# Strassen's form for a layer's last matrix product, and its normalization in pairs of chunks

## The chip, the cores and the metric

The kernel runs on one core of a Trainium2 chip. The metric is the device time of one execution in microseconds (us), as the median of the runs. The engines of the core are TensorE (PE in the profile; PEld is its weight load), VectorE (DVE), ScalarE (ACT), GpSimd (POOL) and SyncE (SP, which here only issues DMAs). Each engine has a queue of its own and works through it in order; engines wait for each other on semaphores.

## The reference, cut to what matters

Four layers run one after the other on an image tensor x of 2 images, 512 channels and 32 x 32 positions, all in float32. Layer 0 is a deformable attention with an MLP, layer 1 an attention over channels with a batch normalization, layer 2 a softmax attention over positions, layer 3 a gate and a non-local block. The change lies in layer 1, in how its output is made and normalized:

```python
K = conv1x1(X, Wq, bq).reshape(b, HEADS, d, n)
Q = conv1x1(X, Wk, bk).reshape(b, HEADS, d, n)
V = conv1x1(X, Wv, bv).reshape(b, HEADS, d, n)
M = jnp.einsum('bhmn,bhen->bhme', K, V)
Out = jnp.einsum('bhme,bhmn->bhen', M, Q)
Out = conv1x1(Out.reshape(b, c, h, w), Wo, bo) + X
mean = Out.mean(axis=(0, 2, 3), keepdims=True)
var = Out.var(axis=(0, 2, 3), keepdims=True)
Out = (Out - mean) * jax.lax.rsqrt(var + EPS)
return Out * gamma[None, :, None, None] + beta[None, :, None, None]
```

There is no softmax in it, so all that acts on X can be folded into one 512 x 512 matrix per image: Out = A X + bias + X.

## The kernel before, in words

x is held in SBUF as four chunks (k, 0 to 3) of 128 channels, each with 2048 columns: image 0's 1024 positions and then image 1's. A matmul takes 128 x 128 weights and 512 columns. It is float32, and the profile has two records for one such matmul. A PSUM bank holds one 128 x 512 result.

Layer 0 ends with the MLP. Its two products already have the form that the change brings to layer 1: helper functions form sums of blocks (`differences` at L967 for the weights, `spreads` at L974 for the activations), `product` (L1090 to L1106) runs seven block products into four banks A to D, and small reader functions take the banks up as they fill. Its last instructions on VectorE are L1161 (a bank is added to x) and L1165 (the last sum into x, with the bias, and with the sums over positions that layer 1 needs).

Layer 1 (L1209 to L1373) then computes, for each image b:

- G, the 512 x 512 matrix X X^T. L1235 transposes 128 positions at a time into PSUM (`pt`), L1240 (VectorE) and L1242 (ScalarE) copy them out by turns (`xt`), L1244 multiplies (`pg`). L1252 to L1257 copy the upper triangle out and mirror it.
- `bvs` from the position sums (L1262, L1270), U = G Wv (matmul L1278, read at L1285), M per head (matmul L1293, read at L1302).
- R from M and Wk (matmul L1316, read at L1317), a bias row (L1319 to L1334), and A = R Wo (matmul L1339, copied at L1342). The five weight matrices wq, wv, wk, wo and wo in another layout (`wot`, `won`) lie in one tile `lw`.
- The last product (L1348): for each of four output chunks o and each of four column blocks t of 512, four matmuls over k into one bank, and L1355 on VectorE, which adds the bias and x and writes x2. These are 64 matmuls.
- The batch normalization: for each chunk, L1363 takes statistics of four column blocks, L1365 joins them, L1367 to L1372 make scale and shift (the square root, L1368, on ScalarE), and L1373 scales the whole chunk in place.

Layer 2 starts with `l2_fg` (L1388, `pf`): for each of two outputs and two column halves, four matmuls over the chunks of the normalized x of image 0, read by ScalarE (L1395). Then `l2_attn` goes over eight tiles of positions: scores (L1421, `pscore`), a maximum (L1432), an exponential (L1435), a scaling (L1436, L1437), transposes (L1441), copies (L1442); `l2_h` (L1407, `ph`) is put between them. L1450 (`pz`) needs all eight tiles.

The queues aren't in the order of the source. When the program is built, a scheduler goes by what is ready and places each instruction in its engine's queue; afterwards that order is fixed. Statistics of one chunk, for instance, come between the sums of the next.

Of the kernel before, what the change touches and what calls it, by code (L numbers as in the profile page):

```python
# [10 lines left out]
F32 = mybir.dt.float32  # L11
AF = mybir.ActivationFunctionType
ALU = mybir.AluOpType
# [3 lines left out]
P = 128  # L17
# [54 lines left out]
def conv_seq(  # L72
# [61 lines left out]
    with ExitStack() as ctx_l0:  # L134
# [459 lines left out]
        with tc.tile_pool(name="hid", bufs=3) as hid, tc.tile_pool(name="sm", bufs=1) as sm, tc.tile_pool(name="hps", bufs=2, space=PSUM) as hps, tc.tile_pool(  # L594
# [6 lines left out]
            def at(n, when, fn, *args):  # L601

                todo.setdefault((n, when), []).append((fn, args))
# [615 lines left out]
    with tc.tile_pool(name="d", bufs=2) as d, tc.tile_pool(name="dpg", bufs=4, space=PSUM) as dpg, tc.tile_pool(  # L1219
# [66 lines left out]
        for b in both:  # L1286

            M[b] = d.tile([P, KC, 2, DH], F32, name="M")
            nc.gpsimd.memset(M[b], 0.0)  # L1289
            pm = dps.tile([P, KC, 2, DH], F32, name="pm", tag="ps")  # L1290
            for o in range(KC):
                for k in range(KC):
                    nc.tensor.matmul(  # L1293
                        pm[:, o].rearrange("p h e -> p (h e)"),
                        lhsT=wq[:, k, o * P : (o + 1) * P],
                        rhs=U[b][:, k, o * P : (o + 1) * P],
                        start=(k == 0),
                        stop=(k == KC - 1),
                    )
                for h in range(2):  # L1300
                    hs = slice(h * DH, (h + 1) * DH)
                    nc.vector.scalar_tensor_tensor(  # L1302
                        M[b][hs, o, h, :],
                        bvs[b][hs, o, h, :],
                        v("L1_conv_bq", o)[hs],
                        pm[hs, o, h, :],
                        ALU.mult,
                        ALU.add,
                    )
        for b in both:  # L1310
            R = d.tile([P, KC, C], F32, name="R")
            prb = dps.tile([P, C], F32, name="prb", tag="ps")
            for o in range(KC):
                mo_ = M[b][:, o].rearrange("p h e -> p (h e)")
                pr = dps.tile([P, C], F32, name="prk", tag="ps")
                nc.tensor.matmul(pr, lhsT=mo_, rhs=wk[:, o, :], start=True, stop=True)  # L1316
                (nc.vector.tensor_copy, nc.scalar.copy)[o % 2](R[:, o, :], pr)  # L1317

                nc.tensor.matmul(  # L1319
                    prb[:, o * P : (o + 1) * P],  # L1320
                    lhsT=v("L1_conv_bk", o).to_broadcast([P, P]),
                    rhs=mo_,
                    start=True,
                    stop=True,
                )
            rb = d.tile([P, C], F32, name="rb")
            nc.scalar.copy(rb, prb)
            bias1[b] = d.tile([P, KC], F32, name="bias1")
            for o in range(KC):
                junk = d.tile([P, C], F32, name="junk", bufs=1)  # L1330
                nc.vector.scalar_tensor_tensor(
                    junk, won[:, o, :], 1.0, rb, ALU.mult, ALU.mult, accum_out=bias1[b][:, o : o + 1]
                )
            nc.vector.tensor_tensor(bias1[b], bias1[b], v("L1_conv_bo"), ALU.add)  # L1334
            A[b] = d.tile([P, KC, C], F32, name="A")
            for i in range(KC):
                pa = dps.tile([P, C], F32, name="pa", tag="ps")
                for k in range(KC):
                    nc.tensor.matmul(  # L1339
                        pa, lhsT=R[:, k, i * P : (i + 1) * P], rhs=wot[:, k, :], start=(k == 0), stop=(k == KC - 1)  # L1340
                    )
                (nc.vector.tensor_copy, nc.scalar.copy)[i % 2](A[b][:, i, :], pa)  # L1342
        for o in range(KC):
            for t in range(NT // 512):
                b, ns = t // 2, slice(t * 512, (t + 1) * 512)
                pr = (dps, dpg)[t % 2].tile([P, 512], F32, name="pr", tag="ps g".split()[t % 2])
                for k in range(KC):
                    nc.tensor.matmul(  # L1348
                        pr,
                        lhsT=A[b][:, k, o * P : (o + 1) * P],  # L1350
                        rhs=x[:, k, ns],
                        start=(k == 0),
                        stop=(k == KC - 1),
                    )
                nc.vector.scalar_tensor_tensor(  # L1355
                    x2[:, o, ns], pr, bias1[b][:, o : o + 1], x[:, o, ns], ALU.add, ALU.add
                )
        x = x2

        for k in range(KC):  # L1360
            st = d.tile([P, NT // 512, nc.vector.BN_STATS_DIM], F32, name="st", bufs=2)
            for t in range(NT // 512):
                nc.vector.bn_stats(st[:, t, :], x[:, k, t * 512 : (t + 1) * 512])  # L1363
            mv = d.tile([P, nc.vector.BN_AGGR_DIM], F32, name="mv", bufs=2)
            nc.vector.bn_aggr(mv, st.rearrange("p t s -> p (t s)"))  # L1365
            sc = d.tile([P, 2], F32, name="sc", bufs=2)
            nc.vector.tensor_scalar(sc[:, 0:1], mv[:, 1:2], EPS, None, ALU.add)  # L1367
            nc.scalar.activation(sc[:, 0:1], sc[:, 0:1], AF.Sqrt)  # L1368
            nc.vector.reciprocal(sc[:, 0:1], sc[:, 0:1])
            nc.vector.tensor_tensor(sc[:, 0:1], sc[:, 0:1], v("L1_conv_gamma", k), ALU.mult)  # L1370
            nc.vector.tensor_tensor(sc[:, 1:2], mv[:, 0:1], sc[:, 0:1], ALU.mult)
            nc.vector.tensor_tensor(sc[:, 1:2], v("L1_conv_beta", k), sc[:, 1:2], ALU.subtract)  # L1372
            nc.vector.tensor_scalar(x[:, k, :], x[:, k, :], sc[:, 0:1], sc[:, 1:2], ALU.mult, ALU.add)  # L1373


    ctx_lw.close()
# [6 lines left out]
    def l2_fg(b, fp, ps):  # L1383
        fg = fp.tile([P, 2, HW], F32, name="fg")
        for i, half in ((0, 0), (0, 1), (1, 0), (1, 1)):
            pf = ps.tile([P, 512], F32, name="pf2", tag="ps")
            for k in range(KC):
                nc.tensor.matmul(  # L1388
                    pf,
                    lhsT=l2w[:, k, i, :],  # L1390
                    rhs=x[:, k, b * HW + half * 512 : b * HW + (half + 1) * 512],
                    start=(k == 0),
                    stop=(k == KC - 1),
                )
            nc.scalar.activation(  # L1395
                fg[:, i, half * 512 : (half + 1) * 512],
                pf,
                AF.Relu,
                bias=l2s[:, 1, 1:2] if i else l2f[:, 1:2],
                scale=l2s[:, 0, 1:2] if i else l2f[:, 0:1],  # L1400
            )
        return fg
# [332 lines left out]
```

## Time and profile before

| what | value |
|---|---|
| median of three runs | 2767.3 us (2765.76 to 2767.45) |
| profiled execution | 2764.49 us |
| its span in the profile | 2762.7 us |
| TensorE busy | 2707.0 us (98%) |
| VectorE busy | 2266.7 us (82%) |
| ScalarE busy | 1544.3 us (56%) |
| mean granted TensorE clock | 0.996 |
| layer 1, from the last L1161 to the end of its product | 2404.35 to 2583.24 us |
| its last product (L1348) | 2528.31 to 2583.24 us |

Times in the profile count from the start of the span. The busy share is an average over the whole program, most of which is layer 0's position bias (the loop of L616); what an edit in layer 1 is worth has to be read from layer 1's own stretch.

### The profile page before, as it was taken

The numbers are of one execution on the slowest core, as the hardware profiler recorded it, in microseconds if no ns is written. First come the engines' busy times: TensorE is split into PE (matmuls) and PEld (weight loads), VectorE is DVE, ScalarE is ACT, GpSimd is POOL, SyncE is SP. The second block draws the span as 40 slices with busy tenths as digits, with TensorE's granted clock in tenths as the row PEclk, the third lists the DMA queues.
The fourth block names the chain that finished last, engine by engine and source line by source line (L and its number), as shares of the span: only waits on it lengthen the run. The fifth ranks groups of instructions, "written<-read, shape, count | busy, mean of one in ns | idle before, by whom it ended". The sixth has DMA issues, their size and how long they took to land.

```text
span 2762.7 us, 49727 instructions
## 1 busy us (share of the span) xinstructions
PE 2707.0 (98%) x19782; PEld 987.5 (36%) x19782; DVE 2266.7 (82%) x2473; ACT 1544.3 (56%) x1950; POOL 663.6 (24%) x776
## 2 busy tenths in 40 slices
PE   8999999999999999999999999999999999999996
PEld 4233323233332323333333333333344444455543
DVE  6999999999999999999999999999654545523555
ACT  6676677667667776766776676676321111001244
POOL 0333333333333333333333333333100000000000
PEclk9999999999999999999999999999999999999998
DMA  3777777777777777777787778777400000100001
GB/s 121 160 163 155 161 154 160 158 160 158 154 164 149 162 163 158 161 161 156 167 185 172 152 165 193 154 170 159 102 30 23 16 23 23 70 7 0 0 1 61
DMA packets 145479, 335.14 MB, mean 121 GB/s; under 512 B 22592, under 2 KB 32064, under 8 KB 144480
## 3 DMA queue, kind: packets, MB, share of 16 engines
q0 software_dynamic: 77824, 201.38, 41.1%
q1 hardware_dynamic: 66992, 130.08, 13.2%
q8 instruction: 156, 2.56, 0.4%
q14 instruction: 75, 0.61, 0.1%
q10 hardware_dynamic: 432, 0.51, 0.1%
HBM read 58.99 MB, written 4.46 MB: 23 GB/s over the span
## 4 chain that ended last, share of the span: by engine, by line
PE 93%; ACT 3%; DVE 2%; issue 1%; DMA 1%; ACTq 0%; DVEq 0%; POOL 0%; SPq 0%; POOLq 0%
PE ph L616 61%; PE A L1101 4%; PE D L1101 4%; PE C L1101 4%; PE psim L669 2%; PE pr L1348 2%; PE B L1101 2%; PE po L1036 2%; PE pg L1244 1%; PE psim L654 1%; PE pz L1450 1%; PE pa L1339 1%; PE pu L1278 1%; ACT r L625 1%; PE pscore L1421 1%
## 5 line engine op out<-in xcount | busy, mean ns | idle before, releaser
L616 PE MATMUL ph<-h,w2a 128*32 128x512 f32 x16384 | 1790.7, 593 | 7.0 <-ACT r L625 6.9
L625 ACT ACTIVATE r<-ph,sb 128x1024 f32<-128x1024 f32 x1024 | 1141.4, 1115 | 562.3 <-PE ph L616 541.1
L349 DVE CUSTOM_DVE_ANT_1 h<-tab 128x1024 f32<-128x1024 f32 x1024 | 1205.9, 1220 | 8.6 <-PE ph L616 4.7
L616 PEld LDWEIGHTS ph<-h,w2a 128*32 128x32 f32 x16384 | 533.5, 109 | 1217.5 <-issue 833.1
L631 DVE SCALAR_TENSOR_TENSOR r<-r,rel,r 128x1024 f32<-128x1024 f32 x512 | 656.0, 1281 | 28.0 <-ACT r L625 27.3
L646 POOL DMA_DIRECT2D xs<-r x512 | 476.9, 1144 | 196.0 <-PE ph L616 95.7
L634 POOL DMA_DIRECT2D r<-r x256 | 222.2, 868 | 1107.2 <-DVE r L631 931.1
L172 ACT ACTIVATE tab<-tab,vec 128x256 f32<-128x256 f32 x252 | 137.1, 544 | 0.0
L1289 POOL MEMSET M<- 128x512 f32 x2 | 1.0, 520 | 439.6 <-DVE x L1165 439.6
L1141 ACT COPY u<-A 128x512 f32<-128x512 f32 x16 | 9.4, 585 | 146.9 <-PE A L1101 146.9
L1120 ACT ACTIVATE h<-h,vec 128x512 f32<-128x512 f32 x32 | 23.1, 721 | 113.6 <-DVE h L1123 113.6
L669 PE MATMUL psim<-xs,cw 128*32 128x512 f32 x512 | 72.1, 592 | 2.1 <-DMA xs<-r 2.1
L1123 DVE TENSOR_TENSOR h<-C,u 128x512 f32<-128x512 f32 x32 | 22.1, 691 | 48.8 <-PE C L1101 48.5
L1101 PE MATMUL A<-xn,w 128*128 128x512 f32 x128 | 60.2, 593 | 0.8 <-DVE x L1043 0.8
L1101 PE MATMUL C<-hT,w 128*128 128x512 f32 x128 | 60.3, 592 | 0.0
L1101 PE MATMUL A<-h,w 128*128 128x512 f32 x128 | 60.1, 592 | 0.0
L1036 PE MATMUL po<-q,vwo 128*128 128x512 f32 x128 | 56.4, 594 | 0.0
L1348 PE MATMUL pr<-x,A 128*128 128x512 f32 x128 | 55.1, 592 | 0.0
L229 DVE SCALAR_TENSOR_TENSOR acc<-q,vec,acc 128x128 f32<-128x128 f32 (+3 forms) x88 | 46.2, 525 | 0.8
L1161 DVE TENSOR_TENSOR x<-D,x 128x512 f32<-128x512 f32 x32 | 22.1, 691 | 26.0 <-PE D L1101 26.0
L852 ACT ACTIVATE e<-e,den 128x64 f32<-128x64 f32 x128 | 41.7, 336 | 2.7 <-DVE den L848 2.7
L1161 DVE TENSOR_TENSOR x<-C,x 128x512 f32<-128x512 f32 x32 | 22.1, 690 | 24.8 <-PE C L1101 24.8
(288 smaller groups left out, 1770.3 us busy)
## 6 DMA issues: line engine op xcount, KB each, us to landing
r<-r POOLq DMA_DIRECT2D x256, 512.0 KB, 4.7
xs<-r SPq DMA_DIRECT2D x512, 128.0 KB, 2.4
xs<-r POOLq DMA_DIRECT2D x512, 128.0 KB, 4.8
tab<-fd SPq DMA_DIRECT2D x63, 512.0 KB, 6.0
lw<-in_l_w_dram SPq DMA_DIRECT2D x5, 1024.0 KB, 10.2
x<-in_x_dram SPq DMA_DIRECT2D x4, 1024.0 KB, 8.5
w<-in_mlp_w_dram SPq DMA_DIRECT2D x8, 512.0 KB, 4.2
w<-in_mlp_w_dram SPq DMA_DIRECT2D x16, 256.0 KB, 3.2
```

What stands on the lines that cost most here:

```text
L172: return nc.scalar.activation(tf, tf if src is None else src[:, :, :, ax, :], AF.Identity, bias=0.0 if ax == 0 else v("L0_conv_cpb_b1"), s ...
L229: pin(nc.vector.scalar_tensor_tensor(dst, src, wt_, dst, ALU.mult, ALU.add))
L349: nc.vector._custom_dve(TENSOR_ADD_SAT, out=h1[:, h], in0=tab[:, j, h, 0, :].unsqueeze(1).to_broadcast([P, 32, 32]), in1=tab[:, j, h, 1, : ...
L616: nc.tensor.matmul(ph[t * 32 : (t + 1) * 32, i, :], lhsT=w2a[:, o], rhs=h1s[2 * p + i][:, h, half * 512 : (half + 1) * 512], start=True, s ...
L625: pin(nc.scalar.activation(r, ph, AF.Relu, bias=sb3[:, o, 1:2]))
L631: pin(nc.vector.scalar_tensor_tensor(r0, r1, rel[:, i : i + 1], r0, ALU.mult, ALU.add))
L634: pin(nc.gpsimd.dma_start(rs[p, 0], rs.pop((p, 2)), accum_op=ALU.add))
L646: pin(nc.gpsimd.dma_start(rs[p][i::2], r[i::2, i, :], accum_op=ALU.add))
L669: nc.tensor.matmul(psims[g, kb][m * 32 : (m + 1) * 32, :], lhsT=cw3[:, 3 - i : 35 - i], rhs=rs.pop(p + m), start=False, stop=(i == 3), ski ...
L1036: nc.tensor.matmul(po, lhsT=vwo[:, k * B + t // 2, o * P : (o + 1) * P], rhs=q[:, k, ts_], start=(k == 0), stop=(k == KC - 1),)
L1101: nc.tensor.matmul(banks[bank], lhsT=a[an][k], rhs=b_[bn_][k], start=(i < 4 and k == 0), stop=(k == n - 1), skip_group_check=True,)
L1348: nc.tensor.matmul(pr, lhsT=A[b][:, k, o * P : (o + 1) * P], rhs=x[:, k, ns], start=(k == 0), stop=(k == KC - 1),)
```

## The change: what it does

For each image, A and X are cut into 2 x 2 blocks: A into blocks of 256 x 256, X into blocks of 256 channels (two chunks) by 512 columns. The four blocks of A X then come from seven block products in place of eight:

- sums of X: T1 = B12 - B11, T2 = B22 - T1, T4 = B21 - T2, T3 = B22 - B12, each 128 x 1024 in SBUF. Image 0's are put into x2's second half, which is free until image 1's results are written; image 1's into the places of wq and wv.
- sums of A, by `differences`: S1 = A21 + A22, S2 = S1 - A11, S4 = A12 - S2, and S3 = A11 - A21 in A21's place. Image 0's go into wk's place, image 1's into won's.
- `layer_out(b, o)` runs one unit of seven products of two matmuls each into four banks, for image b and for output chunks o and o + 2. There are four units, with 56 matmuls in all. Image 0 uses the four banks of one PSUM pool, image 1 those of the other.
- The readers: ScalarE copies the first product to u. VectorE adds the second to u, adds u to three blocks of x (v22, v21, v12), adds the third to v22, and writes the four result blocks with the bias to x2.

The normalization goes by pairs of chunks, (0, 2) and (1, 3), as a unit finishes two chunks at a time. Each scaling is split by image, and chunk 1 of image 0 is given to ScalarE. The first product of layer 2 takes the chunks in the order 0, 2, 3, 1. R now shares its buffers with G, and A with U.

```diff
+        lo, hi = slice(0, 2), slice(2, 4)
+        places = [x2[:, :, HW:], lw[:, 0:2].rearrange("p i k c -> p (i k c)").rearrange("p (n f) -> p n f", n=4)]
+        xblocks = {}
         for b in both:
-            R = d.tile([P, KC, C], F32, name="R")
+            b11, b21, b12, b22 = (
+                x[:, k, b * HW + t * 512 : b * HW + (t + 1) * 512] for t in range(2) for k in (lo, hi)
+            )
+            t1, t2, t3, t4 = (places[b][:, n].rearrange("p (k f) -> p k f", k=2) for n in range(4))
+            nc.vector.tensor_tensor(t1, b12, b11, ALU.subtract)
+            nc.vector.tensor_tensor(t2, b22, t1, ALU.subtract)
+            nc.vector.tensor_tensor(t4, b21, t2, ALU.subtract)
+            nc.vector.tensor_tensor(t3, b22, b12, ALU.subtract)
+            xblocks[b] = {"11": b11, "21": b21, "22": b22, "T1": t1, "T2": t2, "T3": t3, "T4": t4}
+        for b in both:
+            R = d.tile([P, KC, C], F32, name="R", tag="G")
...
-            A[b] = d.tile([P, KC, C], F32, name="A")
+            A[b] = d.tile([P, KC, C], F32, name="A", tag="U")
...
-        for o in range(KC):
-            for t in range(NT // 512):
-                b, ns = t // 2, slice(t * 512, (t + 1) * 512)
-                pr = (dps, dpg)[t % 2].tile([P, 512], F32, name="pr", tag="ps g".split()[t % 2])
-                for k in range(KC):
+        ablocks = {}
+        for b in both:
+            a11, a12, a21, a22 = (A[b][:, k, m] for m in (slice(0, C // 2), slice(C // 2, C)) for k in (lo, hi))
+            s1, s2, s4 = (
+                (wk, won)[b][:, n, :].rearrange("p (k f) -> p k f", k=2) for n in range(3)
+            )
+            differences(a11, a21, a12, a22, s1, s2, s4)
+            ablocks[b] = {"11": a11, "12": a12, "S3": a21, "22": a22, "S1": s1, "S2": s2, "S4": s4}
+
+        def layer_out(b, o):
+            pool, tag = ((dps, "ps"), (dpg, "g"))[b]
+            u = d.tile([P, 512], F32, name="u1")
+            vs = {n: d.tile([P, 512], F32, name=f"v{n}") for n in ("12", "21", "22")}
...
+            def final(n, t, other):
+                k = 2 * (int(n[0]) - 1) + o
+                nc.vector.scalar_tensor_tensor(at(n, x2), t, bias1[b][:, k : k + 1], other, ALU.add, ALU.add)
+
+            def c1(t):
+                plus(u, t, u)
+                for n in ("22", "21", "12"):
+                    plus(vs[n], u, at(n, x))
+
+            banks = {n: pool.tile([P, 512], F32, name=f"pr{n}", tag=tag) for n in "ABCD"}
+            for i, (bank, an, bn_, read) in enumerate(
+                [
+                    ("A", "11", "11", lambda t: nc.scalar.copy(u, t)),
+                    ("B", "S2", "T2", c1),
+                    ("C", "S3", "T3", lambda t: plus(vs["22"], t, vs["22"])),
+                    ("D", "S1", "T1", lambda t: final("22", t, vs["22"])),
+                    ("A", "12", "21", lambda t: final("11", t, at("11", x))),
+                    ("C", "22", "T4", lambda t: final("21", t, vs["21"])),
+                    ("D", "S4", "22", lambda t: final("12", t, vs["12"])),
+                ]
+            ):
+                for k in range(2):
                     nc.tensor.matmul(
-                        pr,
-                        lhsT=A[b][:, k, o * P : (o + 1) * P],
-                        rhs=x[:, k, ns],
-                        start=(k == 0),
-                        stop=(k == KC - 1),
+                        banks[bank],
+                        lhsT=ablocks[b][an][:, k, o * P : (o + 1) * P],
+                        rhs=xblocks[b][bn_][:, k, :],
+                        start=(i < 4 and k == 0),
+                        stop=(k == 1),
+                        skip_group_check=True,
                     )
-                nc.vector.scalar_tensor_tensor(
-                    x2[:, o, ns], pr, bias1[b][:, o : o + 1], x[:, o, ns], ALU.add, ALU.add
-                )
+                read(banks[bank])
+
+        for b in both:
+            for o in range(2):
+                layer_out(b, o)
         x = x2
 
-        for k in range(KC):
+        for ks in ((0, 2), (1, 3)):
+            scs = {}
+            for k in ks:
...
-            nc.vector.tensor_scalar(x[:, k, :], x[:, k, :], sc[:, 0:1], sc[:, 1:2], ALU.mult, ALU.add)
+            for b in both:
+                for k in ks:
+                    xs = x[:, k, b * HW : (b + 1) * HW]
+                    if (b, k) == (0, 1):
+                        nc.scalar.activation(xs, xs, AF.Identity, bias=scs[k][:, 1:2], scale=scs[k][:, 0:1])
+                    else:
+                        nc.vector.tensor_scalar(xs, xs, scs[k][:, 0:1], scs[k][:, 1:2], ALU.mult, ALU.add)
...
-            for k in range(KC):
+            for j, k in enumerate((0, 2, 3, 1)):
                 nc.tensor.matmul(
                     pf,
                     lhsT=l2w[:, k, i, :],
                     rhs=x[:, k, b * HW + half * 512 : b * HW + (half + 1) * 512],
-                    start=(k == 0),
-                    stop=(k == KC - 1),
+                    start=(j == 0),
+                    stop=(j == KC - 1),
                 )
```

More of the change, by code (lines that the diff above doesn't have):

```diff
@@ new lines, in conv_seq, with at, plus @@
+        for b in both:
[9 more added lines that the diff above has]
+            vs = {n: d.tile([P, 512], F32, name=f"v{n}") for n in ("12", "21", "22")}
+            def at(n, of):
+                m, t = int(n[0]) - 1, int(n[1]) - 1
+                return of[:, 2 * m + o, b * HW + t * 512 : b * HW + (t + 1) * 512]
+            def plus(to, t, other):
+                nc.vector.tensor_tensor(to, t, other, ALU.add)
+            def final(n, t, other):
[18 more added lines that the diff above has]
+                for k in range(2):
+                    nc.tensor.matmul(
+                        banks[bank],
[4 more added lines that the diff above has]
+                        skip_group_check=True,
+                    )
+                read(banks[bank])
@@ L1358, in conv_seq @@
+        for b in both:
+            for o in range(2):
+                layer_out(b, o)
         x = x2
-        for k in range(KC):
[L1361 to L1373, printed above, removed]
+        for ks in ((0, 2), (1, 3)):
+            scs = {}
+            for k in ks:
+                st = d.tile([P, NT // 512, nc.vector.BN_STATS_DIM], F32, name="st", bufs=4)
+                for t in range(NT // 512):
+                    nc.vector.bn_stats(st[:, t, :], x[:, k, t * 512 : (t + 1) * 512])
+                mv = d.tile([P, nc.vector.BN_AGGR_DIM], F32, name="mv", bufs=4)
+                nc.vector.bn_aggr(mv, st.rearrange("p t s -> p (t s)"))
+                sc = scs[k] = d.tile([P, 2], F32, name="sc", bufs=4)
+                nc.vector.tensor_scalar(sc[:, 0:1], mv[:, 1:2], EPS, None, ALU.add)
+                nc.scalar.activation(sc[:, 0:1], sc[:, 0:1], AF.Sqrt)
+                nc.vector.reciprocal(sc[:, 0:1], sc[:, 0:1])
+                nc.vector.tensor_tensor(sc[:, 0:1], sc[:, 0:1], v("L1_conv_gamma", k), ALU.mult)
+                nc.vector.tensor_tensor(sc[:, 1:2], mv[:, 0:1], sc[:, 0:1], ALU.mult)
+                nc.vector.tensor_tensor(sc[:, 1:2], v("L1_conv_beta", k), sc[:, 1:2], ALU.subtract)
+            for b in both:
[5 more added lines that the diff above has]
+                        nc.vector.tensor_scalar(xs, xs, scs[k][:, 0:1], scs[k][:, 1:2], ALU.mult, ALU.add)
```

## The prediction

> **What bounds the kernel now.** I read the head of the page, the chain that ended last and the costliest groups; then busy time by stage; then the timeline at the three places where the change puts work.
>
> ```profile
> span 2762.7 us, 49727 instructions
> ...
> PE 93%; ACT 3%; DVE 2%; issue 1%; DMA 1%; ACTq 0%; DVEq 0%; POOL 0%; SPq 0%; POOLq 0%
> ...
> L1101 PE MATMUL A<-xn,w 128*128 128x512 f32 x128 | 60.2, 593 | 0.8 <-DVE x L1043 0.8
> ...
> L1348 PE MATMUL pr<-x,A 128*128 128x512 f32 x128 | 55.1, 592 | 0.0
> ...
> L1161 DVE TENSOR_TENSOR x<-D,x 128x512 f32<-128x512 f32 x32 | 22.1, 691 | 26.0 <-PE D L1101 26.0
> ```
>
> TensorE carries 93% of the chain. L1348 is the product that changes: 64 float32 matmuls, two records each, with no idle time ahead of them. L1101, layer 0's MLP in the same seven-product form, runs its 128 records at the same pace, and its vector sums take 691 ns each.
>
> Busy time by stage (columns: window, its length, then PE, PEld, DVE, ACT, POOL) ahead of, in, and after the product, up to layer 2's first pz:
>
> ```profile
> 2404.35:2528.30 123.95, 122.39 (x444) 69.88 (x445) 33.17 (x70) 12.54 (x25) 0.98 (x2) 1.00 0.11 43
> 2528.30:2583.24 54.94, 54.94 (x129) 24.32 (x128) 28.48 (x51) 2.48 (x5) 0.00 (x0) 1.00 0.00 0
> 2583.24:2629.07 45.83, 43.50 (x193) 26.13 (x192) 22.19 (x41) 21.49 (x37) 0.00 (x0) 1.00 0.00 0
> ```
>
> In the product TensorE has no gap at full clock, while VectorE is busy for 28.5 of 54.9 us. So matmuls taken out shorten the stage, as long as VectorE keeps up.
>
> The timeline at layer 1's start (start, duration, engine; in brackets the idle time and who ended it):
>
> ```profile
> 2404.35 0.69 DVE L1161 TENSOR_TENSOR x<-D,x 128x512 f32<-128x512 f32 x1 [0.23 <-PE D L1101]
> ...
> 2405.07 0.75 DVE L1165 SCALAR_TENSOR_TENSOR x<-vs,vec,x 128x512 f32<-128x512 f32 x1
> 2405.09 1.53 PE L1235 MATMUL pt<-cst,x 128*128 128x128 f32 x12 [0.78 <-DVE x L1161]
> ...
> 2405.95 1.30 ACT L1242 COPY xt<-pt 128x512 f32<-128x512 f32 x2 [24.18 <-DVE x L1165]
> ...
> 2406.58 6.74 PE L1244 MATMUL pg<-xt 128*128 128x512 f32 x24
> ```
>
> ScalarE's first copy xt waits for the MLP's last L1165, and TensorE's pg for that copy.
>
> The timeline where the product ends:
>
> ```profile
> 2583.24 4.45 PE L1388 MATMUL pf<-x,l2w 128*128 128x512 f32 x10
> 2587.86 9.71 PE L1388 MATMUL pf<-x,l2w 128*128 128x512 f32 x22 [0.16 <-DVE x L1373]
> ...
> 2583.45 0.75 DVE L1355 SCALAR_TENSOR_TENSOR x<-pr,bias,x 128x512 f32<-128x512 f32 x1 [1.95 <-PE pr L1348]
> ...
> 2586.46 1.35 DVE L1373 TENSOR_SCALAR x<-x,sc 128x2048 f32<-128x2048 f32 x1
> ```
>
> Only chunk 3's normalization is left at that point, and pf on chunks 0 to 2 covers it but for about 0.3 us.
>
> The timeline at the end of layer 2's first attention:
>
> ```profile
> 2622.54 1.88 PE L1421 MATMUL pscore<-fg 128*128 128x512 f32 x4
> 2624.26 1.05 PE L1407 MATMUL ph<-l2w,x 128*128 128x128 f32 x8
> 2626.61 1.06 PE L1441 MATMUL pt<-cst,e 128*128 128x128 f32 x8 [1.29 <-DVE e L1437]
> 2628.17 1.07 PE L1441 MATMUL pt<-cst,e 128*128 128x128 f32 x8 [0.50 <-DVE e L1437]
> 2629.07 13.90 PE L1450 MATMUL pz<-at,ht 128*128 128x512 f32 x32
> ```
>
> From the last score to pz it is 4.8 us: a maximum, an exponential and a scaling in a row, with little for TensorE to do.
>
> [...] 128x1024 takes 1220 ns at L1590 and 750 ns at L1437. [...] so an early sum delays what stands behind it; the L1242 copy above shows who then waits. [...] so the one normalization given to ScalarE after Sqrt loads no table. The trace of before agrees for Relu: after Sqrt's load at 2529.11 (1.28 us) the next is at 2598.40, for the exponential.
>
> **The change part by part**, with the order in which the changed program was built.
>
> *Matmuls.* One takes 54.95/64 = 0.8585 us. 64 become 4 units of 14, 56 in all: 48.08 us. Saved: 6.87.
>
> *The image sums of b=0 (L1321 to L1324 of the changed kernel).* Four tensor_tensor of 128x1024, 1.22 each. They aren't placed beside the product but at layer 1's start: the first right after the L1161 of 2404.35, ahead of the last L1165, the second behind that. Consecutive vector instructions overlap by 0.08 (L1373 at 2558.99 lasts 1.35, the next starts at 2560.26), so L1165 comes 1.14 later, the xt copy at about 2407.1, pg at 2407.7. TensorE meanwhile does one tile of four transposes more (4 x 0.107 = 0.43), so 0.7 is lost. The second copy xt (VectorE, done at 2409.2) is in time for pg's second tile (2409.9); the other two sums stand where VectorE sits idle for 6.9 us. Bounds: 0.3 to 1.2 (all of the delay, uncovered).
>
> *The image sums of b=1*, into used wq and wv. One stands before the last U, in a 2.7 us gap. One waits for the last pm that reads wq; behind it are the last M pair and, with two more sums between, both R copies, each later by about 2 us. R's first copy ends at 2495.8, pa starts at 2496.5; the second ends at 2497.8, its matmul comes at 2498.2. Nothing lost, with 0.4 us of cover; past that each us costs one.
>
> *The sums of A.* Four of 128x512 (0.69) per image, in used wk and won. Image 0's wait for A and for prk's reads of wk; behind them stands an R copy, ending at 2514.8 where 2516.3 is needed. Image 1's start after the last copy of A (2529.1), end at 2531.9, just as VectorE is wanted for the first bank B, and TensorE is by then in image 0's banks. Nothing lost.
>
> *The reads of the products.* A unit has 5 tensor_tensor of 0.69, 4 scalar_tensor_tensor of 0.75 and 4 bn_stats of 0.69: 9.2 us in 12.02 of matmuls, and ScalarE one copy (0.59). Bank A is written again 5.2 us after its first product ends, and ScalarE copies it at once; C and D after 3.4: VectorE reads C behind four sums, done 6.9 us into the unit where the second product into C starts at 8.6. Nothing lost; PSUM banks aren't shared by the images.
>
> *The tail.* With E the end of the product: the last unit has on top four normalizations of 128x1024 (0.75) and eight small instructions, so its last sum starts at E+0.9 instead of E+0.2. Then three bn_stats and two aggregates (to E+4.1), Sqrt and the scale and shift of two chunks (0.12 to 0.2 each, to E+5.5), then chunk 1 of b=0 on ScalarE (nearest row L1587, 1.15; L1589 with a pointer scale, 1.19): done near E+6.8. TensorE has six pf matmuls on chunks 0 and 2 (5.15) and one ph (0.21), to E+5.4; next in its queue is ph on chunk 1, ahead of pf on chunk 3. It waits 1.4 us where before waited 0.3: 1.1 lost; bounds 0.5 (VectorE on time) to 1.9.
>
> *The attention behind it.* The new order sets tile 5's and 6's transposes into the middle of the last score product, so from the last score on only one ph (0.89) and one tile of transposes (0.87) lie in the same 4.8 us: idle 3.0 where before had 1.3 + 0.5. Small waits before it even out to about -0.2: 1.0 lost; bounds 0 to 2.
>
> No DMA is added, and POOL's and SP's queues are as before. Sum: -6.87 + 0.7 + 1.1 + 1.0 = -4.1. The profiled execution took 2764.49 (span 2762.7 and 1.8 around it): 2760.4, span 2758.6. The median of the runs is 2.8 above it: **2763.2**. A difference of under 0.2% (5.5 us) is about what a measurement of this kernel can't tell from none, and 4.1 is under that.
>
> **Rivals.**
> *A: the saving is kept nearly whole* (tail and attention cost nothing): 6.87 - 0.7 = 6.2, 2761.1. For: VectorE has 2.8 us free per unit, and the old tail was covered. Against: E+6.8 against E+5.4.
> *B: the tail eats more*: a wait of 3 us at ph and 2 in the attention, gain 1.6, 2765.7. For: the scale chain is all small dependent steps, and now two are interleaved. Against: the same steps took 3.0 us from sum to normalization before.
> *C: slower; VectorE becomes the bound of the product.* Its 13 instructions per unit average 0.71 us. TensorE waits from 0.92 each, the gain is gone at 1.0; at 1.2 a unit lasts 15.6 instead of 12.0: 14.4 lost, 2777.6. For: the sums now have SBUF operands on both sides while bn_stats shares the queue. Against: L1161 and L1363 hold 0.69 with TensorE at full pace.
>
> **How the numbers follow.** My forecast (2761.8 to 2764.8 by itself) 0.60, A 0.20, B 0.13, C 0.07. The range 2760.3 to 2766.0 takes in A and B and leaves out C and the ends. Faster by over 0.2% (below 2761.8): A and an edge of mine, 0.24. Slower (above 2772.8): C, 0.06. Within: 0.70.
>
> **What would show it.** Right: L1403 with 112 records in 48.1 us and no idle ahead; pg about 1.1 later against L1161; a TensorE idle of 1 to 2 us at ph released by ScalarE's L1437; one of about 3 before the last transposes. Wrong: idle ahead of L1403 released by VectorE (C), or pf running through (A); R copies late for pa would cost more than I allowed.

## The result, and the profile after

| | before | after |
|---|---|---|
| median, 20 runs each | 2766.81 us | 2761.86 us |
| lowest to highest | 2765.57 to 2768.14 | 2759.11 to 2765.84 |
| profiled execution, span | 2764.49, 2762.7 | 2765.84, 2764.0 |

The ratio of the medians is 0.9983, with a 95% interval of 0.9977 to 0.9989: the change saves 4.95 us, which is under 0.2% and still clear of none. I had forecast 4.1, a time of 2763.2 in a range of 2760.3 to 2766.0. Two things in this table are not in the forecast. The runs after spread over 6.7 us, those before over 2.6. And the profiled execution of after is the slowest of its 20: it is longer than the profiled one of before, although the kernel is faster. So stages have to be compared first.

Busy time by stage of the kernel after (columns as in the prediction): from layer 0's last sum to the product, the product, and from its end to the first pz.

```profile
2407.53:2532.22 124.69, 122.53 (x445) 69.88 (x445) 44.41 (x82) 12.46 (x25) 0.98 (x2) 1.00 0.11 43
2532.22:2580.28 48.06, 48.06 (x113) 21.28 (x112) 37.94 (x67) 4.51 (x8) 0.00 (x0) 1.00 0.00 1
2580.28:2628.56 48.28, 44.01 (x194) 27.07 (x192) 25.05 (x53) 23.32 (x39) 0.00 (x0) 0.97 0.00 1
```

Against before's 123.95, 54.94 and 45.83 these are +0.74, -6.88 and +2.45. The product is as forecast (48.08), and VectorE, 37.9 of 48.1 us busy, never makes TensorE wait in it. In the last row the granted clock is 0.97; none of before's three stages had less than 1.00. Outside of these stages layer 0 ends 3.18 us later (2407.53 against 2404.35), and pz itself takes 2.16 us more. With 0.35 less at the program's end these make up the 1.3 us by which the span is longer.

The timeline at layer 1's start:

```profile
2407.53 0.69 DVE L1161 TENSOR_TENSOR x<-D,x 128x512 f32<-128x512 f32 x1 [0.23 <-PE D L1101]
2408.14 1.21 DVE L1321 TENSOR_TENSOR x<-x 128x1024 f32<-128x1024 f32 x1
2409.27 0.74 DVE L1165 SCALAR_TENSOR_TENSOR x<-vs,vec,x 128x512 f32<-128x512 f32 x1
...
2410.13 1.07 ACT L1242 COPY xt<-pt 128x512 f32<-128x512 f32 x2 [25.19 <-DVE x L1165]
...
2410.77 1.12 PE L1244 MATMUL pg<-xt 128*128 128x512 f32 x2 [0.53 <-ACT xt L1242]
```

The first sum of X, L1321, stands ahead of the MLP's last L1165 in VectorE's queue, and L1165 starts 1.74 us behind L1161, where before it was 0.72; ScalarE's copy waits for that L1165 and TensorE's pg for the copy. From L1161 to pg it is 3.24 us; before it was 2.23.

The timeline at the product's end, E = 2580.28:

```profile
2580.28 5.31 PE L1454 MATMUL pf<-x,l2w 128*128 128x512 f32 x12
2581.04 0.74 DVE L1383 SCALAR_TENSOR_TENSOR x<-prD,bias,v 128x512 f32<-128x512 f32 x1
...
2584.80 0.27 DVE L1432 TENSOR_TENSOR sc<-vec,sc 128x1 f32<-128x1 f32 x2
2584.98 1.24 ACT L1437 ACTIVATE x<-x,sc 128x1024 f32<-128x1024 f32 x1 [0.69 <-DVE sc L1432]
...
2586.28 0.71 PE L1473 MATMUL ph<-l2w,x 128*128 128x128 f32 x4 [0.46 <-ACT x L1437]
```

ph does wait for ScalarE's normalization of chunk 1, as forecast, but not by 1.4 us: the list has 0.46, and by the starts of the matmuls 0.64 are lost (the list leaves out the overlap of 0.17 with the matmul before), where before had 0.16 in the list and 0.33 by the starts.

The timeline at the end of the first attention, and the stretches of 2 us there (the third figure from the right is the granted clock):

```profile
2622.17 1.02 PE L1487 MATMUL pscore<-fg 128*128 128x512 f32 x2
2623.03 1.05 PE L1473 MATMUL ph<-l2w,x 128*128 128x128 f32 x8
2626.82 1.94 PE L1507 MATMUL pt<-cst,e 128*128 128x128 f32 x8 [2.74 <-DVE e L1503]
2628.56 16.06 PE L1516 MATMUL pz<-at,ht 128*128 128x512 f32 x32
```

```profile
2624.00:2626.00 2.00, 0.08 (x1) 0.00 (x0) 0.89 (x4) 1.21 (x2) 0.00 (x0) 1.00 0.01 4
2626.00:2628.00 2.00, 1.18 (x6) 1.21 (x7) 0.68 (x1) 0.05 (x1) 0.00 (x0) 0.52 0.00 0
...
2632.00:2634.00 2.00, 2.00 (x5) 0.92 (x4) 0.00 (x0) 0.00 (x0) 0.00 (x0) 0.78 0.00 0
```

The idle time of 2.74 us is there as forecast. From about 2626.1, inside this gap, the clock is at half for 6.8 us, as worked out from these stretches (the two left out show 0.50): the last transposes take 1.94 us instead of 1.06, and pz 16.06 instead of 13.90. That is 3.0 us which I hadn't counted. The same happens at 46 us, in layer 0, behind a gap of 2.21 us which the kernel before has as well. The transposes behind it, before and after:

```profile
45.83 1.26 PE L412 MATMUL pt<-cst,xn 128*128 128x128 f32 x8 [2.21 <-DVE x L413]
46.43 1.97 PE L412 MATMUL pt<-cst,xn 128*128 128x128 f32 x8 [2.21 <-DVE x L413]
```

After, the clock is at half from about 45.6 to 52.4 us (0.50 in each of the three stretches from 46 to 52, 0.90 and 0.89 in those around them). Of layer 0's 3.18 us, 0.60 are there already when these transposes start, 0.43 of them in TensorE's first wait for its weights (6.43 us against 6.00); the fall costs the other 2.6.

Putting the end of layer 0 where before has it and taking out the 3.0 leaves a span of 2764.0 - 3.2 - 3.0 = 2757.8, or 2759.6 with the 1.8 around it. I call this the undisturbed time; it is an estimate, good to about half a microsecond. The profiled execution of before shows no such fall, so its 2764.5 is undisturbed already. The last 20 to 25 us of the program are left out of this: there the profiles of before and of after both have the clock at half for most of the time. It falls inside an idle time of 11.2 us, about 1.5 us behind its start in before and 0.6 in after, and the stretches wholly inside the fall show 0.50.

### The profile page after: what moved, and what is told of

The parts are those of the page before. It is cut to its first block, busy times and chain, and to the rows that moved or that the text cites. A ratio compares the mean times of both kernels' runs of the same rounds, so it can differ in the third digit from the quotient of the medians.

```text
span 2764.0 us, 49761 instructions
## 1 busy us (share of the span) xinstructions
PE 2705.4 (98%) x19766; PEld 986.3 (36%) x19766; DVE 2290.1 (83%) x2512; ACT 1548.6 (56%) x1955; POOL 662.7 (24%) x776
## 4 chain that ended last, share of the span: by engine, by line
PE 92%; DVE 3%; ACT 3%; issue 1%; DMA 1%; ACTq 0%; DVEq 0%; POOL 0%; SPq 0%; POOLq 0%
PE ph L616 61%; PE A L1101 4%; PE D L1101 4%; PE C L1101 4%; PE psim L669 2%; PE B L1101 2%; PE po L1036 2%; PE pg L1244 1%; PE pz L1516 1%; PE psim L654 1%; PE pa L1355 1%; PE pu L1278 1%; ACT r L625 1%; PE pscore L1487 1%; DVE h L349 1%
## 5 line engine op out<-in xcount | busy, mean ns | idle before, releaser
L1161 DVE TENSOR_TENSOR x<-D,x 128x512 f32<-128x512 f32 x32 | 22.1, 690 | 26.0 <-PE D L1101 26.0
L1161 DVE TENSOR_TENSOR x<-C,x 128x512 f32<-128x512 f32 x32 | 22.1, 690 | 24.8 <-PE C L1101 24.8
L1244 PE MATMUL pg<-xt 128*128 128x512 f32 (+3 forms) x128 | 36.4, 439 | 1.4 <-ACT xt L1242 1.1
## 6 DMA issues: line engine op xcount, KB each, us to landing
lw<-in_l_w_dram SPq DMA_DIRECT2D x5, 1024.0 KB, 10.1
```

The costliest lines, as they stand in the source:

```text
L1244: nc.tensor.matmul(pgs[i], lhsT=xt[:, i * P : (i + 1) * P], rhs=xt[:, i * P :], start=(t == 0), stop=(t == 7),)
```

## The experiments

Each kernel is the kernel after with the edit shown. Beside its median stands that of the kernel before on the same chip.

### Where the saving comes from: the pairs without Strassen

```diff
-            for i, (bank, an, bn_, read) in enumerate([... seven products ...]):
+            for n in ("11", "12", "21", "22"):
+                bank = pool.tile([P, 512], F32, name=f"pr{n}", tag=tag)
+                for k in range(KC):
+                    nc.tensor.matmul(bank, lhsT=A[b][:, k, c * P : (c + 1) * P], rhs=x[:, k, ns], ...)
+                final(n, bank, at(n, x))
```

> The pairs without Strassen: the last product in the order of the changed kernel's units, but by eight block products (64 matmuls), without any sums of X or of A; pairs of chunks, image-wise scaling and pf order as in the changed kernel. In its built order the first attention has its last score product whole again, as the kernel before has. Theory (the whole gain is the 8 matmuls; the hand-off, the tail and the attention's order only take from it): product 54.9 us, last L1161 to the product 124.0, idle ahead of the last transposes about 1.8 in all, the time 2766.8 give or take 0.6, equal to before's, with before's narrow spread. Rival (the pairs themselves cost or bring something): over 1 us away from 2766.8.

Measured: 2765.67 us (13 runs, 2764.12 to 2767.2), before 2766.0; ratio 1.0000 (0.9992 to 1.0008). The same three stages of this kernel:

```profile
2404.42:2528.38 123.96, 122.41 (x445) 69.88 (x446) 33.16 (x70) 12.55 (x25) 0.98 (x2) 1.00 0.11 43
2528.38:2583.31 54.93, 54.93 (x129) 24.32 (x128) 28.33 (x53) 3.72 (x6) 0.00 (x0) 1.00 0.00 0
2583.31:2628.73 45.42, 43.24 (x194) 26.21 (x192) 22.39 (x42) 21.51 (x37) 0.00 (x0) 1.00 0.00 0
```

The first two are before's to 0.01 us; the third is 0.41 shorter, since pf on its pairs of chunks never waits here. The attention has before's two short gaps (1.30 and 0.50 us) and no fall of the clock. The 2766.8 of the theory was before's median in the first table; here before itself has 2766.0, and the two are equal to within the interval. So the pairs alone change nothing that the medians can tell, and the whole saving comes from the product of seven. The hand-off, the late tail and the attention's new order come with it too: this kernel has none of the three.

### The hand-off

```diff
+            if b == 0:
+                nc.gpsimd.tensor_copy(x2[:, :, HW : HW + 1], G[0][:, :, 0:1])
             nc.vector.tensor_tensor(t1, b12, b11, ALU.subtract)
```

> The changed kernel with image 0's four sums of X held back until image 0's G is finished (a copy of one column of G by GpSimd into the place of each sum goes ahead of them). Theory (the two sums around the MLP's last L1165 cost the hand-off 0.73 us): from the last L1161 to the product 124.0 us in place of 124.69, the time 0.7 better: about 2761.1. Rival (the sums only move the delay, since they now stand between the copies xt of image 1): 124.7 or more, no gain.

Measured: from the last L1161 (2403.44) to the product (2527.33) 123.89 us:

```profile
2403.44:2527.33 123.89, 122.34 (x444) 69.83 (x445) 44.80 (x82) 12.55 (x25) 1.18 (x3) 1.00 0.11 43
```

The 0.8 is back, and what the sums delay between the xt copies of image 1 is hidden. The median, 2761.77 (21 runs, before 2766.0), doesn't show it: this kernel still has the gap of 2.74 us, and its own profile has the fall of the clock behind it. A gain of 0.8 us can be read from the stage, not from medians of runs that spread over 5 us.

### How much cover VectorE has in the product

The first attempt had the added sums inside the loop over the seven products, so that there were 147 instead of 21; they also change u while it is still in use, so it computes something else.

```diff
                 read(banks[bank])
+                if (b, o) != (1, 1):
+                    for _ in range(7):
+                        nc.vector.tensor_tensor(u, u, at("11", x), ALU.add)
```

> The changed kernel with seven more vector sums (128x512, 0.69 each; they add x to the used u and nobody reads it) behind each of the first three units of the last product: 21 x 0.69 = 14.5 us more on VectorE. Theory (VectorE has in this stage some 49 us and fills about 44 of them; the rest is cover): 14.5 - 5 = 9.5 us late at the end of the last sum, so some 2771; TensorE waits at banks of image 1. Rival (VectorE's cover is only the 2.8 us per unit of each unit, or a bank is read late much earlier): 14 us or more, 2776.

Measured: 2845.33 us, which decides nothing between the numbers above, as those were for 21 sums. It is of use all the same. VectorE issues these sums every 0.60 us, though each is listed with 0.69: 147 x 0.60 = 88.2, less the 10.1 us that VectorE has idle in the product of after (48.06 - 37.94), is 78.1. From the product's start to the end of chunk 1's normalization it took 131.3 us instead of 54.0, 77.3 more.

With the sums behind the loop, 21 of them:

```diff
                 read(banks[bank])
+            if (b, o) != (1, 1):
+                for _ in range(7):
+                    nc.vector.tensor_tensor(u, u, at("11", x), ALU.add)
```

> The changed kernel with seven more vector sums (128x512, unused results) behind each of the first three units of the last product, 21 in all and this time outside the loop over the seven products. Theory (VectorE issues such sums every 0.60 us and has 10.1 us idle in the product): 12.6 of work against 10.1 of cover: from the product's start to the first pscore 65.7 to 66.5 us in place of 63.2. Rivals: cover of 5 us only, 70.8 or more; no cover, 75.8.

Measured: from the product's start to the first pscore 64.8 us in place of 63.2, in one execution. The product's stage, and the first pf behind it:

```profile
2531.57:2579.64 48.07, 48.07 (x113) 21.09 (x111) 46.63 (x83) 4.61 (x8) 0.00 (x0) 1.00 0.00 0
```

```profile
2581.91 5.39 PE L1457 MATMUL pf<-x,l2w 128*128 128x512 f32 x12 [2.11 <-DVE sc L1434]
```

With 12.6 us more to do VectorE is busy for 46.6 of 48.1 us, and no matmul of the product waits; what doesn't fit comes out as a wait of 2.11 us at pf. The cover is some 10 to 11 us over the product, near the 2.8 us per unit (11.3 over four) that the prediction worked out for VectorE; the theory was 0.9 too high, its two rivals 6 and more. So VectorE was as far from being the product's bound as the prediction had it, and C failed for that reason.

This run shows another thing by chance. The order built for its attention had the last score product whole again:

```profile
2624.53 1.06 PE L1510 MATMUL pt<-cst,e 128*128 128x128 f32 x8 [0.37 <-DVE e L1506]
2626.18 1.06 PE L1510 MATMUL pt<-cst,e 128*128 128x128 f32 x8 [0.58 <-DVE e L1506]
```

Two gaps of 0.37 and 0.58, no fall of the clock (1.00 from 2618 to 2634), and from pscore to pz 30.7 us in place of 33.15 (32.3 without the clock's part). It gets back in the attention what it loses in the tail: from the product's end to pz 47.44, as after without the clock's part (47.44; the runs with the filled gap below have that too). The edit also moved the tail, so this is a sign of what the order is worth, and no test of it alone.

### The tail

```diff
-                    if (b, k) == (0, 1):
-                        nc.scalar.activation(xs, xs, AF.Identity, bias=scs[k][:, 1:2], scale=scs[k][:, 0:1])
-                    else:
-                        nc.vector.tensor_scalar(xs, xs, scs[k][:, 0:1], scs[k][:, 1:2], ALU.mult, ALU.add)
+                    nc.vector.tensor_scalar(xs, xs, scs[k][:, 0:1], scs[k][:, 1:2], ALU.mult, ALU.add)
```

> The changed kernel with chunk 1 of image 0 normalized on VectorE like the others instead of on ScalarE. Theory (the wait at ph ends with the scale and shift at 4.8 us behind the product's end, whichever engine scales): ph's wait all but gone, then pf waits some 0.3 for chunk 3, which is 0.7 later on VectorE: from the product's end to the first pscore 14.8 in place of 15.13 us. Rival (ScalarE's 1.24 us is the whole of the tail's cost): 14.5.

Measured: 14.98 us in place of 15.13, in one execution. ph's wait is gone, and pf's weight load now waits 0.20 us for chunk 3. Neither number is hit: 0.15 are saved, not 0.3 or 0.6. Giving that chunk to ScalarE is worth nothing here; the tail hangs on the scale and shift, which are ready at E + 4.8 either way. This execution had the gap of 2.74 us and no fall of the clock behind it (1.00 in every stretch of 2 us from 2618 to 2634):

```profile
2622.79 1.07 PE L1504 MATMUL pt<-cst,e 128*128 128x128 f32 x8 [2.74 <-DVE e L1500]
```

Its span was 2757.3: the undisturbed time that I had worked out, less the 0.15, to within 0.4.

### The gap in the attention and the clock

First the kernel after itself once more, with new runs.

> The changed kernel unaltered, on the chip and in the rounds of the runs beside it, as their anchor. Theory (the granted clock falls behind the 2.74 us gap of the first attention): its profile shows pz or the transposes ahead of it longer than 13.9 and 1.06 us, and its median lies about 3.5 us above what its own profile gives without any fall of the clock (2759.6), as with the two kernels that had this gap before. Rival (chance alone): 1.7 above it, as with the kernels that had no such gap.

Measured: 2762.12 us (21 runs, 2759.5 to 2765.32), before 2766.39; ratio 0.9984 (0.9977 to 0.9990). In its profile the last transposes take 1.94 us and pz 16.07. The median lies 2.5 above 2759.6, between what the two theories gave, so it doesn't tell them apart; the profile does speak for the first. At 46 us it has a fall of 3.4 us, where after had 6.8 (mean clock 0.83 and 0.66 from 44 to 54 us). From the transposes at 46 us to the product's end it takes 2534.1 us all the same, after 2533.9; so it lost more somewhere between, by an estimate about 1.5 us (half of after's 2.6, and these 0.2). And like the profiled execution of after it is among the slowest of its kind (the second of 21), so these two lost more than the usual execution does.

Work put into the gap (the bank is read by nobody):

```diff
+                def between(t):
+                    l2_h(0, t, ht, psh, "h")
+                    if t == 7:
+                        warm = psh.tile([P, 512], F32, name="warm", tag="h")
+                        for k in range(2):
+                            nc.tensor.matmul(warm, lhsT=l2w[:, k, 2, :], rhs=x[:, k, :512], start=True, stop=True)
```

> The changed kernel with two more matmuls of 128x512 (four records, 1.72 us; their bank is read by nobody) on TensorE, behind the last ph of the first image and ahead of its last tile of transposes, where the changed kernel has 2.74 us of idle time. Theory (the idle time makes the granted clock fall in a part of the executions, about 3.0 us each time): no fall behind the last transposes, pz 13.9 us, the executions bunch as before's do, the median is about 2759.6 (the 2757.8 of an undisturbed span and 1.8 around it), so 2 us better than the changed kernel's 2761.9. Rival (the clock falls by chance or from something earlier, the gap has no part in it): the median stays at 2761.9 and the runs still spread over 6 us.

Measured: 2761.31 us (21 runs, 2759.03 to 2762.78), before 2766.0. The end of its first attention:

```profile
2622.88 1.98 PE L1671 MATMUL warm<-x,l2w 128*128 128x512 f32 x4 [0.62 <-DVE ht L1480]
2625.00 1.06 PE L1507 MATMUL pt<-cst,e 128*128 128x128 f32 x8
2625.90 13.90 PE L1516 MATMUL pz<-at,ht 128*128 128x512 f32 x32
```

No fall: pt and pz have their old durations, and the highest run is 2.5 us lower than that of the run before. But the median is 4.7 us under before's, where after had 4.95 and, the second time, 4.3. So it shows no gain at all, let alone the 2 of the theory, and on that count the rival wasn't beaten here. The runs do lie closer together, over 3.8 us in place of 6.7 and 5.8. The profile still has a fall at 46 us (0.62 and 0.53 in the two stretches of 2 us from 46 to 50), and the mean of 0.94 over its first 60 us is lower than the 0.97 that this fall alone would leave.

The gap made longer:

```diff
             nc.vector.tensor_scalar(e2, e2, den, None, ALU.mult)
+            if b == 0 and t == 7:
+                for _ in range(2):
+                    nc.vector.tensor_scalar(e2, e2, 1.0, None, ALU.mult)
```

> The changed kernel with two more scalings by 1.0 (128x1024, 0.75 each) on VectorE for the first image's last tile, so that the 2.74 us of idle time ahead of the last transposes become about 4.2. Theory (the idle time makes the clock fall): the clock falls in nearly every execution: 2759.6 + 1.5 + 3.0 = 2764.1 or more, and no run under 2763. Rival (it falls by chance): every run is 1.5 later than the changed kernel's, the fastest about 2760.6, the median 2763.4, the spread 6 us as there.

Measured: 2764.49 us (13 runs, 2762.01 to 2767.05), before 2766.0; the profile has the fall:

```profile
2626.28 1.51 PE L1510 MATMUL pt<-cst,e 128*128 128x128 f32 x8 [4.20 <-DVE e L1506]
```

The median is near that of the theory (2764.1 or more; the rival had 2763.4), but two runs are under its floor of 2763. So the fall isn't certain even behind 4.2 us, or it is shorter in some executions: here the transposes and pz lost 1.74 us, in after 3.0.

The split score product undone, by giving the score matmuls precedence in the order:

```diff
-            for half in range(2):
-                nc.tensor.matmul(pscore[:, half, :], ...)
+            with tc.high_priority():
+                for half in range(2):
+                    nc.tensor.matmul(pscore[:, half, :], ...)
```

> The changed kernel with the score matmuls of layer 2 given precedence when the order is built, so that the first image's last score product is whole again and two tiles of transposes and two ph stand behind it. Theory (the split score product makes the long gap): no gap above 2 us ahead of the last transposes, no fall of the clock there, from the product's end to pz about 46.1 us in place of 48.28 (0.87 of these were clock), the median about 2759.9. Rival (the idle time only moves to another wait of the attention): 47.4 us, and a median of 2761.2 where the clock stays up.

Measured: 2765.61 us (13 runs), before 2766.39, so the gain is gone. The last gap shrinks to 0.56 us and the clock stays up, but from the product's end to pz it is 48.06 us: ph now waits for its bank before nearly every tile (up to 1.12 us). Here the rival was right that the idle time moves, and the loss is larger than its 47.4. The edit also reached image 1's attention, and from pz to the end it is 136.8 us instead of 133.6. As an undoing of the order it was too coarse; the run with 21 sums says more of it.

The two fillers together, the second in layer 0's gap:

```diff
                 for t in range(NT // 512):
+                    if (k, t) == (3, 2):
+                        pd = aps.tile([P, 512], F32, name="pq")
+                        for j in range(2):
+                            pin(nc.tensor.matmul(pd, lhsT=qw[:, j, :], rhs=xn[j][:, :512], start=True, stop=True))
                     flip_x(k, t, dve)
```

> The changed kernel with the two idle-filling matmuls in the first attention and two more of 128x512 in the 2.21 us gap of TensorE at 43.6 us, at the program's start (a gap that the kernel before has too); nobody reads the banks. Theory (idle time of over 2 us makes the granted clock fall, at the start in part of the executions, in the attention in most): both falls are gone, the median comes down from 2762 to the 2759.6 of an undisturbed execution, and the runs lie within 1.5 us. Rival (the falls at the start are chance and not from that gap): 2761.3 and a spread of 4 us, as with the attention's filler alone.

Measured: 2759.64 us (11 runs, 2759.11 to 2761.85), before 2765.68. The transposes behind layer 0's gap, with the filler:

```profile
45.89 1.25 PE L412 MATMUL pt<-cst,xn 128*128 128x128 f32 x8 [0.49 <-DVE x L413]
```

The median is the undisturbed time to 0.1 us, with matmuls added that compute nothing. It is 6.0 under before's; the ratio of 0.998 (0.997 to 0.9989) has an interval that overlaps after's, so by the medians alone this gain over after isn't clear. Its profile shows a clock of 1.00 at both places (from 30 to 54 and from 2620 to 2660 us), a span of 2758.1, and 124.69, 48.07 and 47.44 us in the three stages. Seven of the 11 runs lie within 0.8 us; the other four are up to 2.2 above, so the 1.5 us of the theory were not kept.

What those four have is on record, as each execution comes with its mean granted clock: the seven have 0.996, the four 0.995. The same sorts the other runs. After's six executions with 0.996 lie at 2759.11 to 2760.05, its 14 with 0.994 or 0.995 at 2760.72 to 2765.84. Of before's 105 executions beside these runs 13 have 0.996, with a median of 2764.1, and the other 92 lie at 2765.28 or more. So in both kernels the executions whose clock stayed up are the fast ones. (Between 0.994 and 0.995 before's times aren't sorted; three decimals are coarse for that, as a fall of 3.4 us changes the mean by 0.0006.) The lowest runs of after, with one filler and with both are 2759.11, 2759.03 and 2759.11: the fillers make no execution faster than after's undisturbed ones. Both together leave fewer that are disturbed (4 of 11, where after has 14 of 20 and 20 of 21); the one in the attention alone doesn't (19 of 21).

### Real work in the gap

```diff
+                def between(t):
+                    l2_h(0, t, ht, psh, "h")
+                    if t == 7:
+                        l2_fg(1, fp, psh, fg1, ((0, 0),), "h")
...
-                fg = l2_fg(1, fp, ps)
+                fg = l2_fg(1, fp, ps, fg1, ((0, 1), (1, 0), (1, 1)))
```

(with the sums held back as above)

> The changed kernel with image 0's sums of X held back until G is finished, and with the first of image 1's four pf results (four matmuls, 3.43 us) computed in the gap ahead of the first image's last transposes, in ph's bank, instead of behind pz. Theory (TensorE's own work fills the gap): the last transposes come 1.3 later, no fall of the clock there, 3.43 - 1.3 = 2.1 us kept: without falls of the clock 2756.1, as a median with the usual 1.6 about 2757.7. Rival (the pf taken out was covering waits of the non-local block): no more than 0.5 kept besides the clock, about 2759.3.

Measured: 2756.75 us (5 runs, 2756.11 to 2760.29), before 2766.39; ratio 0.9968 (0.9956 to 0.9981). From the product's end to pz it is 48.85 us, 1.4 more than after without the clock's part, and from pz to the end 129.9 instead of 133.6: 2.3 are kept, where 2.1 were expected. With layer 0's gap filled too:

> Three edits on the changed kernel: image 0's sums of X held back until G is finished, the first of image 1's pf results in the gap of the first attention, and two idle-filling matmuls in the gap at 43.6 us. Theory: no fall of the clock at either place, so the median equals the undisturbed 2756.3, some 10 us under the kernel before, spread under 1.5 us. Rival (the gap at the start has no part): 2757.5 and single runs up to 2760.

Measured: 2756.14 us (5 runs, four of them within 0.3 us, one at 2758.46), before 2765.68; ratio 0.9966 (0.9954 to 0.9979). That is 9.5 us faster than before, nearly twice what the change brought. Against the run without layer 0's filler the two intervals overlap; that filler is shown by the run with both fillers, not here.

## Why the prediction was right, and where not

- **The matmuls**: -6.87 forecast, -6.88 measured, and no wait on VectorE. The run with eight products shows that nothing else in the change saves time that the medians can tell.
- **The hand-off**: 0.7 forecast, 0.74 measured, by the chain named (L1321, L1165, xt, pg; pg 1.01 later, 1.1 forecast), and gone when the sums come later.
- **The image sums, the sums of A, the R copies**: nothing forecast, and nothing seen: pa and the product start without a wait. ScalarE loaded no table for its normalization either, as forecast: after's loads, 1.28 us each, stand at 2570.79 ahead of L1428 and at 2596.41 ahead of L1501, and the normalization (L1437) runs between them at 2584.98.
- **The tail**: this term was mis-sized. I gave 1.1, it cost 0.64 against 0.33 before: 0.3. The mechanism was right, though the wait of 0.46 is not the 1 to 2 us that I had named as its sign. TensorE came to the wait at E + 5.5, near the 5.4 of the prediction; but the last sum started at E + 0.8 (0.9), the aggregates were done at E + 3.6 (4.1) and chunk 1 was normalized at E + 5.9 (6.8). I added up durations. Instructions of VectorE that don't need each other's results overlap: three statistics took 1.87 us, not 3 x 0.69. Each pair of small steps took about 0.2; before, with one chunk, a single step already stands 0.20 behind the one whose result it needs (L1370 to L1372 at 2558.41, 2558.61 and 2558.80), so the second chunk's steps fit in between. I had the overlap of 0.08 in my own working for the hand-off and left it out here.
- **The attention**: the idle time was about right (3.0 forecast from the last score on, 2.74 in the list), and its order cost 1.30 (47.44 - 45.83, less the tail's 0.31), where I gave 1.0. The run with 21 sums, whose order is the old one, agrees with this. What I missed is that so long a gap can cost more than its length. The clock took 3.0 us behind it in both profiled executions of after, 1.36 with the sums late and 1.74 behind the longer gap, and nothing with all of the normalization on VectorE. That fall was not in the bounds.
- **The sum**: undisturbed, -6.88 + 0.74 + 0.31 + 1.30 = -4.5, against -4.1 forecast. Three other numbers agree: the profile with both gaps filled (2758.1 against before's 2762.7, 4.6), the medians of the executions with a clock of 0.996 (2759.7 against 2764.1, 4.4), and the lowest runs (2759.11 against 2763.45, 4.3). The 0.35 us that the profiled execution of after gains behind pz is not the change's: the profiles with one filler, with both, and with all of the normalization on VectorE have 133.6 us there, as before has. Most of the 0.35 lies in the last transposes of the program, in its stretch at half clock: they took 3.48 us instead of 3.75.
- **The step from profile to median**: I put 2.8 us on the profiled time because before's median lay that far above its profile, and didn't ask what these 2.8 were. They are executions with a lower clock, as the clocks on record show. At which gap before loses it is open: the one profile of before holds no fall ahead of the end (1.00 in every stretch of 20 us up to 2720), and it has idle times of 1.94, 2.21 and 2.12 us that end at 14.8, 46 and 1958 us. After's median lies 2.3 above its undisturbed time, about as far as before's, though after has the longer gap in the attention as well. That it came out alike was luck.

So the forecast came close in part because an overestimate (the tail, 0.8) was partly made up by an underestimate (the attention, 0.3), and because an allowance of unknown origin fitted. Rival A had the tail nearly right and the attention wrong; B had the attention's size about right, with the clock, and the tail wrong (its own terms give a gain of 1.5, not 1.6); C failed.

## What to carry to other kernels

In this kernel an idle time of TensorE of 2 us or more had to be priced at its length and a possible fall of the clock behind it: where the profiles show one behind 2.21 or 2.74 us of idle time and its cost could be read, that was 1.36 to 3.0 us. So look at the granted clock in windows of 2 us behind each such gap, and at the mean clock of each execution; where falls are found, put independent work into the gap first. A stage's cover on another engine is its idle time in that stage, and chains of small instructions are priced by the distance of their starts, not by their durations. When a stage gets shorter, read the built order of the stages behind it as well: here one score product was split and the longest gap came of it.

## What the runs showed of the hardware

- The falls of the clock come in two lengths. The full windows of 2 us inside them show 0.50, so a fall's length is estimated from the windows as share lost x length / 0.5. Those in the attention last 6.8 us in both profiled executions of after and 3.4 us in the runs with the longer gap and with late sums; at 46 us there are 6.8 us in the first execution of after and in the runs with 21 and with 147 sums, and 3.4 in the second of after and in four other runs (one filler, the longer gap, the scores first, real work in the gap). Why the same gap of 2.74 us cost 3.0 us, 1.36 or nothing is not shown here.
- Falls stood behind gaps of little more than 2 us. The one of 2.74 us had a fall in both profiled executions of after and in the run with late sums, and none with all of the normalization on VectorE; the one at 46 us (2.21 us in before and after) had one in eight of the twelve profiled executions in which it wasn't filled. But length alone doesn't decide: those other four had none, the gap of 2.11 us in the run with 21 sums had none, and in before and after there was none behind the 2.12 and 2.10 us that end at 1958 and 1961 us, nor behind the 1.94 and 1.95 that end at about 15. The last matmuls ahead of the gaps at 46 us and in the attention are of 128 columns or fewer but for one score product, those ahead of the gaps at 1958 us and in the run with 21 sums are of 512; no run tested whether that has a part in it.
- Longer gaps had falls too: the 4.20 us of the run with the longer gap (0.50 from 2628 to 2630 us) and the 11.2 us near the end of before and after (0.50). In the product of the run with 147 sums, with gaps up to 10.94 us, the mean clock was 0.77. There (the last matmuls ahead of a gap, and those behind it):

```profile
2557.93 1.88 PE L1403 MATMUL prD<-lw 128*128 128x512 f32 x4
2570.74 3.65 PE L1403 MATMUL prC<-x,A 128*128 128x512 f32 x4 [10.94 <-DVE v L1379]
```

Four records that took 1.88 us ahead of the gap took 3.65 behind its 10.94 us of idle time, and 3.78 behind one of 6.04.
